# Attention with two passes: the maxima of later queries in the steps of the exponentials

## The chip, the cores and the metric

The kernel runs on one core of a Trainium2 chip. A core has a matrix engine (TensorE, PE in the profile), VectorE (DVE), ScalarE (ACT), GpSimd (POOL) and SyncE (SP, which only starts transfers here), each with its own stream of instructions; they work on an on-chip buffer, and TensorE writes to an accumulation memory of eight banks (PSUM) that VectorE and ScalarE read. The metric is the device time of one execution in microseconds (us), the median of some runs.

## The reference

Four layers, each a residual: group normalization of x, a mixing layer, and x plus its result. Only layer 0 is touched. x is (4, 96, 56, 56) in float32: four images of 96 channels and L = 3136 places.

```python
# layer 0, on tokens = normalized x as (4, 3136, 96); 3 heads of 16 dimensions
qkv = tokens @ w_qkv.T
q, k, v = ...                                    # (4, 3, 3136, 16) each
attn = softmax(einsum('bhnd,bhmd->bhnm', q, k) * 96 ** -0.5, axis=-1)
out = einsum('bhnm,bhmd->bhnd', attn, v)         # (4, 3, 3136, 16)
out = out.reshape(4, 3136, 48) @ w_proj.T + b_proj
```

Layers 1 and 3 are selective scans over image directions, layer 2 is an attention over windows. They are the larger part of the time, and their code is the same in both kernels.

## The kernel before, in words

`layer0` holds four images at once: image b lives on partitions 32b to 32b + 31 (`rows[b]`) of `qa` (queries) and `ka` (keys), as 16 dimensions and a row of ones in `ka`. Lines 136 to 153 load each image, normalize it (`group_norm`, lines 88 to 110) and compute the values of all heads into `va`, with ones beside them so that the sum of the weights comes out of the same product.

For each of the 3 heads there are then two stages, each with a PSUM pool of its own.

The stage of maxima (lines 160 to 196) first projects queries and keys in 7 chunks of 448 places (line 167). ScalarE takes the queries out of PSUM, VectorE the keys (171, 172), and POOL fills the row of ones (174). Then, for each of 25 tiles of 128 queries (the last has 64) and each of 7 chunks of 448 keys, four products (line 181, one per image) fill four banks, two to a tile `s`, and two reductions on VectorE (line 186) take the maximum over two banks each. Such a pair of a tile and a chunk is called a unit here: 175 per head. After seven units line 191 takes the maximum of the chunks into columns 0, 32, 64 and 96 of a cleared square (`mp`, cleared by POOL in line 190), a product with the identity (193) turns these columns into rows, and line 194 subtracts them from the query's row that meets the ones of the keys. From then on every score comes with its maximum taken away.

The stage of exponentials (lines 197 to 249) goes through 7 chunks of queries and 25 tiles of keys, 175 steps per head. A step has four score products (line 202, keys by queries, one bank per image, six banks in the pool), four exponentials on ScalarE (218) and four products with the values (223) that gather into one bank `acc`, image b on partitions `rows[b]`. After 25 steps lines 230 to 235 copy `acc`, spread the sums by a product with `perm`, take reciprocals and multiply. In the last head, lines 239 to 249 also apply the output projection for each image (three products, line 243), add bias and input, and store, both transfers on SP's queue.

All of this is written in program order. What runs beside what is decided by a scheduler that keeps the order of the program as priority, and by the buffers of the pools. `in_order` (line 54), which other layers use, chains the instructions of each engine in the order in which they are written.

Of the kernel before, what the change touches and what calls it, by code (L numbers as in the profile page):

```python
# [9 lines left out]
F32 = mybir.dt.float32  # L10
AF = mybir.ActivationFunctionType
ALU = mybir.AluOpType
AX = mybir.AxisListType
PSUM = bass.MemoryType.PSUM
# [3 lines left out]
L = H * W  # L18
# [13 lines left out]
def view(ap, offset, dims):  # L32

    return bass.AP(ap.tensor, ap.offset + offset, [ap.ap[0], *dims])
# [35 lines left out]
class Net:  # L70
# [41 lines left out]

    def layer0(self, xin, xout):

        nc, tc = self.nc, self.tc
        scale = C ** -0.5
        n128 = [(t * 128, min(128, L - t * 128)) for t in range((L + 127) // 128)]
        rows = [slice(32 * b, 32 * b + 32) for b in range(B)]
        with ExitStack() as cx:
            wp = cx.enter_context(tc.tile_pool(name="l0w", bufs=1))  # L120
            s1 = cx.enter_context(tc.tile_pool(name="l0b", bufs=1))
            ss = cx.enter_context(tc.tile_pool(name="l0s", bufs=2))
            psA = cx.enter_context(tc.tile_pool(name="l0pA", bufs=1, space=PSUM))
            psM = cx.enter_context(tc.tile_pool(name="l0pM", bufs=1, space=PSUM))
            wq, wk, wv, wo, bo, perm = (
                self.load(wp, n) for n in ("l0_wq", "l0_wk", "l0_wv", "l0_wo", "l0_bo", "k_perm")
            )

            def misc():
                return psM.tile([128, 512], F32, name="misc")  # L130

            xns = []

            va = s1.tile([128, len(n128), HEADS, B, 2 * HD], F32, name="va")
            nc.gpsimd.memset(va, 1.0)
            for b in range(B):
                x = s1.tile([C, L], F32, name="x")
                nc.sync.dma_start(x, xin[b])
                xn = s1.tile([C, L], F32, name=f"xn{b}")
                self.group_norm(x, xn, ss, psM, "misc")  # L140
                xns.append(xn)
                for t0 in range(0, len(n128), 8):
                    some = n128[t0 : t0 + 8]
                    n = some[0][1]
                    p = misc()
                    for i, (k0, nk) in enumerate(some):
                        nc.tensor.matmul(
                            p[:nk, i * 48 : (i + 1) * 48], xn[:, k0 : k0 + nk], wv, start=True, stop=True
                        )
                    nc.vector.tensor_copy(  # L150
                        va[:n, t0 : t0 + len(some), :, b, 0:HD],
                        p[:n, : 48 * len(some)].rearrange("p (t h d) -> p t h d", h=HEADS, d=HD),
                    )
            aos = []
            for h in range(HEADS):

                qa = s1.tile([128, L], F32, name="qa")
                ka = s1.tile([128, L], F32, name="ka")
                ao = s1.tile([128, L], F32, name=f"ao{h}")
                aos.append(ao)  # L160
                with tc.tile_pool(name="l0p1", bufs=3, space=PSUM) as ps:
                    for c in range(NCH):
                        cs = slice(c * CH, (c + 1) * CH)
                        p = ps.tile([128, 2, 512], F32, name="s")
                        for i, w in enumerate((wq, wk)):
                            for b in range(B):
                                nc.tensor.matmul(
                                    p[rows[b], i, :CH], w[:, 32 * h : 32 * h + 32], xns[b][:, cs],
                                    start=True, stop=True,
                                )  # L170
                        nc.scalar.copy(qa[:, cs], p[:, 0, :CH])
                        nc.vector.tensor_copy(ka[:, cs], p[:, 1, :CH])
                    for b in range(B):
                        nc.gpsimd.memset(ka[32 * b : 32 * b + 1, :], 1.0)  # L174

                    for q0, nq in n128:
                        pm = ss.tile([128, B, NCH], F32, name="pm")
                        for kc in range(NCH):
                            two = [ps.tile([128, 2, 512], F32, name="s") for _ in range(2)]
                            for b in range(B):  # L180
                                nc.tensor.matmul(  # L181
                                    two[b // 2][:nq, b % 2, :CH], qa[rows[b], q0 : q0 + nq],
                                    ka[rows[b], kc * CH : (kc + 1) * CH], start=True, stop=True,
                                )
                            for i in range(2):
                                nc.vector.tensor_reduce(  # L186
                                    pm[:nq, 2 * i : 2 * i + 2, kc], two[i][:nq, :, :CH], AX.X, ALU.max
                                )
                        mp = ss.tile([128, 128], F32, name="mp")
                        nc.gpsimd.memset(mp, 0.0)  # L190
                        nc.vector.tensor_reduce(view(mp[:nq], 0, [[32, B]]), pm[:nq], AX.X, ALU.max)
                        p = misc()
                        nc.tensor.matmul(p[:, :nq], mp[:nq, :], self.ident[:nq, :nq], start=True, stop=True)
                        nc.vector.tensor_tensor(
                            qa[:, q0 : q0 + nq], qa[:, q0 : q0 + nq], p[:, :nq], ALU.subtract
                        )
                with tc.tile_pool(name="l0p2", bufs=6, space=PSUM) as ps:

                    def scores(qc, k0, nk):
                        four = [ps.tile([128, 512], F32, name="s") for _ in range(B)]  # L200
                        for b in range(B):
                            nc.tensor.matmul(  # L202
                                four[b][:nk, :CH], ka[rows[b], k0 : k0 + nk],
                                qa[rows[b], qc * CH : (qc + 1) * CH], start=True, stop=True,
                            )
                        return four

                    todo = [(qc, t) for qc in range(NCH) for t in range(len(n128))]
                    s = scores(0, *n128[0])
                    for at, (qc, t) in enumerate(todo):  # L210
                        cs = slice(qc * CH, (qc + 1) * CH)
                        nk = n128[t][1]
                        if t == 0:
                            acc = psA.tile([128, 512], F32, name="acc")
                        es = []
                        for b in range(B):
                            e = ss.tile([128, CH], F32, name="e", bufs=8)
                            nc.scalar.activation(e[:nk], s[b][:nk, :CH], AF.Exp, scale=scale)  # L218
                            es.append(e)
                        if at + 1 < len(todo):  # L220
                            s = scores(todo[at + 1][0], *n128[todo[at + 1][1]])
                        for b in range(B):
                            nc.tensor.matmul(  # L223
                                acc[rows[b], :CH], va[:nk, t, h, b, :], es[b][:nk],
                                start=t == 0, stop=t == len(n128) - 1,
                            )
                        if t < len(n128) - 1:
                            continue
                        a = ss.tile([128, CH], F32, name="a")
                        nc.vector.tensor_copy(a, acc[:, :CH])  # L230
                        p = misc()
                        nc.tensor.matmul(p[:, :CH], perm, a, start=True, stop=True)
                        rc = ss.tile([128, CH], F32, name="rc")
                        nc.vector.reciprocal(rc, p[:, :CH])
                        nc.vector.tensor_tensor(ao[:, cs], a, rc, ALU.mult)
                        if h < HEADS - 1:
                            continue
                        for b in range(B):
                            x = ss.tile([C, CH], F32, name="xc")
                            nc.sync.dma_start(x, xin[b][:, cs])  # L240
                            p = misc()
                            for i in range(HEADS):
                                nc.tensor.matmul(
                                    p[:C, :CH], wo[rows[b], i, :], aos[i][rows[b], cs],
                                    start=i == 0, stop=i == HEADS - 1,
                                )
                            xo = ss.tile([C, CH], F32, name="xo")
                            nc.vector.scalar_tensor_tensor(xo, p[:C, :CH], bo, x, ALU.add, ALU.add)
                            nc.sync.dma_start(xout[b][:, cs], xo)


    def into_scan(self, xin, dram, orders):
# [1272 lines left out]
```

## Time and profile before

| what | value |
|---|---|
| median of 3 runs | 17090.54 us (17080.33 to 17101.61) |
| profiled execution | 17096.45 us |
| its span | 17094.7 us |
| granted TensorE clock, mean over the span | 0.877 of full speed |
| busy: PE, DVE, ACT, POOL | 78%, 82%, 72%, 45% of the span |
| line 186 (DVE), 1050 reductions | 1075.1 us, 1084 ns each |
| line 218 (ACT), 2100 exponentials | 975.8 us, 549 ns in the mean |
| line 181 (PE), 4200 rows | 1087.5 us, 922 ns each |

The span is the time from the first to the last instruction of one profiled execution. In the rows of a profile a float32 product appears as two matmul instructions, so the 4200 rows of line 181 are 2100 products. The matmuls' ends are modelled, and they overlap: the time between the starts of two groups says more about TensorE's pace than the length of a row. A row names output and inputs (`s<-ka,qa`), their shapes and the number of instructions merged into it. The granted clock is the share of its full clock that TensorE was given.

### The profile page before, as it was taken

The numbers are of one execution on the slowest core, as the hardware profiler recorded it, in microseconds if no ns is written. First come the engines' busy times: TensorE is split into PE (matmuls) and PEld (weight loads), VectorE is DVE, ScalarE is ACT, GpSimd is POOL, SyncE is SP. The second block draws the span as 40 slices with busy tenths as digits, with TensorE's granted clock in tenths as the row PEclk, the third lists the DMA queues.
The fourth block names the chain that finished last, engine by engine and source line by source line (L and its number), as shares of the span: only waits on it lengthen the run. The fifth ranks groups of instructions, "written<-read, shape, count | busy, mean of one in ns | idle before, by whom it ended". The sixth has DMA issues, their size and how long they took to land.

```text
span 17094.7 us, 498049 instructions
## 1 busy us (share of the span) xinstructions
PE 13251.9 (78%) x220632; PEld 8905.3 (52%) x220632; DVE 13981.4 (82%) x13756; ACT 12242.0 (72%) x16242; POOL 7703.0 (45%) x4069
## 2 busy tenths in 40 slices
PE   8999992777777777777777667838888888888844
PEld 4333430666666666666666444516666656666622
DVE  7271806999999999999999677768888888888887
ACT  0607063999999999999999234438888888888822
POOL 0000002988888888888888000003333333333300
PEclk6969685999999999999999578959999999999966
DMA  0000003343444444334444830032222212212122
GB/s 13 1 1 1 1 20 133 93 96 89 96 103 105 107 97 94 91 91 102 101 107 101 196 79 12 10 82 50 50 50 52 50 49 51 49 49 50 45 64 65
DMA packets 823179, 1152.29 MB, mean 67 GB/s; under 512 B 309360, under 2 KB 731408, under 8 KB 809248
## 3 DMA queue, kind: packets, MB, share of 16 engines
q1 hardware_dynamic: 763680, 1067.42, 25.7%
q10 hardware_dynamic: 53312, 38.55, 1.0%
q8 instruction: 1734, 28.41, 0.7%
q0 software_dynamic: 4032, 14.46, 0.3%
q14 instruction: 421, 3.45, 0.1%
HBM read 842.93 MB, written 277.18 MB: 66 GB/s over the span
## 4 chain that ended last, share of the span: by engine, by line
DVE 35%; PE 25%; ACT 17%; issue 15%; DMA 4%; POOL 2%; SPq 0%; DVEq 0%; ACTq 0%; POOLq 0%
DVE q L463 17%; PE q L1156 6%; DVE pm L186 6%; ACT ht L488 5%; PE s L202 4%; DVE cv L333 3%; ACT e L451 3%; PE acc L223 3%; ACT phi L1104 2%; PE z L1096 2%; DVE w L1144 2%; ACT w L1112 2%; PE t L386 2%; PE y L500 2%; PE t L479 1%
## 5 line engine op out<-in xcount | busy, mean ns | idle before, releaser
L443 POOL TENSOR_TENSOR q<-du,bm 128x1792 f32<-128x1792 f32 x1344 | 5348.8, 4026 | 2.9 <-DMA bm<-bc 2.9
L463 DVE TENSOR_TENSOR_SCAN q<-e,state,q 128x448 f32<-128x448 f32 x4608 | 4873.9, 1121 | 143.7 <-ACT e L451 142.0
L451 ACT ACTIVATE e<-dl,na 128x448 f32<-128x448 f32 x5376 | 3355.4, 640 | 177.2 <-DVE q L463 120.9
L500 PE MATMUL y<-ht,cd 128*32 128x64 f32 x75264 | 1837.2, 225 | 1479.4 <-ACT ht L488 1478.6
L479 PE MATMUL t<-ident,q 128*128 128x128 f32 x18816 | 2610.7, 292 | 93.8 <-issue 77.7
L1156 PE MATMUL q<-w,m 32*32 32x192 f32 x52224 | 2582.7, 348 | 116.3 <-DVE phi L1165 67.8
L479 PEld LDWEIGHTS t<-ident,q 128*128 128x128 f32 x18816 | 2377.1, 203 | 324.9 <-issue 202.1
L488 ACT COPY ht<-t 128x896 f32<-128x896 f32 x2688 | 2428.3, 903 | 88.9 <-PE t L479 59.5
L500 PEld LDWEIGHTS y<-ht,cd 128*32 128x32 f32 x75264 | 1399.8, 110 | 1956.2 <-ACT ht L488 1942.2
L1156 PEld LDWEIGHTS q<-w,m 32*32 32x32 f32 x52224 | 1876.4, 113 | 733.9 <-issue 163.3
L1165 DVE TENSOR_TENSOR phi<-q,phi 128x768 f32<-128x768 f32 x1632 | 1512.4, 951 | 549.7 <-PE q L1156 535.4
L1177 POOL TENSOR_TENSOR t<-t 128x384 f32<-128x384 f32 x408 | 407.2, 998 | 3002.5 <-DVE t L1176 2996.4
L218 ACT ACTIVATE e<-s 128x448 f32<-128x448 f32 (+1 forms) x2100 | 975.8, 549 | 1055.3 <-PE s L202 1025.2
L1096 PE MATMUL z<-ad,sm 32*32 32x256 f32 x39168 | 1278.5, 391 | 396.9 <-ACT phi L1104 382.7
L1104 ACT COPY phi<-z 128x1536 f32<-128x1536 f32 x816 | 1164.5, 1427 | 538.9 <-PE z L1096 538.9
L1144 DVE TENSOR_TENSOR w<-w,misc 128x3072 f32<-128x3072 f32 x408 | 1364.8, 3345 | 83.6 <-PE misc L1128 46.3
L1112 ACT ACTIVATE w<-phi,lntiny,w_k_rmask 128x3072 f32<-128x3072 f32 x408 | 1203.1, 2949 | 2.6
L186 DVE TENSOR_REDUCE pm<-s 128x2 f32<-128x896 f32 (+1 forms) x1050 | 1075.1, 1084 | 117.2 <-PE s L181 117.2
L1120 ACT ACTIVATE phi<-phi,w_k_nmask 128x3072 f32<-128x3072 f32 x408 | 1165.5, 2857 | 2.4
L181 PE MATMUL s<-ka,qa 32*128 32x448 f32 (+1 forms) x4200 | 1087.5, 922 | 22.2 <-POOL ka L174 17.6
L1096 PEld LDWEIGHTS z<-ad,sm 32*32 32x32 f32 x39168 | 709.0, 105 | 659.8 <-ACT phi L1104 466.6
L230 DVE COPY a<-acc 128x448 f32<-128x448 f32 x21 | 13.1, 624 | 997.5 <-PE acc L223 997.5
(250 smaller groups left out, 17464.3 us busy)
## 6 DMA issues: line engine op xcount, KB each, us to landing
bm<-bc SPq DMA_DIRECT2D x896, 448.0 KB
cm<-cd SPq DMA_DIRECT2D x544, 186.0 KB
l1y<-out SPq DMA_DIRECT2D x672, 96.0 KB
l1y<-out SPq DMA_DIRECT2D x672, 72.0 KB
y<-l1y ACTq DMA_DIRECT2D x224, 168.0 KB
l3y<-y SPq DMA_DIRECT2D x1616, 23.2 KB
w<-l3cr SPq DMA_DIRECT2D x408, 48.0 KB
l3cr<-phi SPq DMA_DIRECT2D x408, 48.0 KB
```

What stands on the lines that cost most here:

```text
L186: nc.vector.tensor_reduce(pm[:nq, 2 * i : 2 * i + 2, kc], two[i][:nq, :, :CH], AX.X, ALU.max)
L443: nc.gpsimd.tensor_tensor(q, spread(s["du"][:, j, :], ng), s["bm"][g], ALU.mult)
L451: nc.scalar.activation(e[:, :CH], s["dl"][:, j, :], AF.Exp, scale=na[:, s["k"], j, n : n + 1])
L463: nc.vector.tensor_tensor_scan(a, e, a, first, ALU.mult, ALU.add)
L479: nc.tensor.transpose(flat(t)[:, 128 * c : 128 * c + 128], view(q, h * NC2 + c, [[NC, 128]]), self.ident,)
L488: nc.scalar.copy(t, flat(s["t", j, g, h])[:, : NC2 * 128])
L500: nc.tensor.matmul(s["y", j][r : r + 32, c // 4, 64 * half : 64 * half + 64], s["cd"][:, half, g, c, :], s["t", j, g, h][:, 128 * i + 64 * ...
L1096: nc.tensor.matmul(z[32 * b : 32 * b + 32, p, dh].rearrange("p n d -> p (n d)"), s["s"][ps_, dh, b, lo : lo + 32], st["ad"][ps_, dh, 8 * h ...
L1112: nc.scalar.activation(w.rearrange("p a n d -> p (a n d)"), st["phi"].rearrange("p a b n d -> p (a b n d)"), AF.Sigmoid, bias=lntiny, scal ...
L1144: nc.vector.tensor_tensor(st["w"], st["w"], ut, ALU.mult)
L1156: nc.tensor.matmul(qp[bs, n, :DI], st["m"][bs, 4 * q + n, :], st["w"][bs, :, 4 * q + n, :], start=True, stop=True,)
L1165: nc.vector.tensor_tensor(ph, view(st[q], 0, [[256, 4], [32, 6], [1, 32]]), ph, ALU.mult)
```

## The change

Both stages of a head become one sequence of steps that runs through all heads. `units` lists the units (head, tile of queries, chunk of keys) and `steps` the steps (head, chunk of queries, tile of keys), 525 of each. The loop takes unit number i in the same turn as step number i - 32 (`LEAD`), so 32 turns have units alone, and the last 32 steps have no units. A turn has two halves. In the first, images 0 and 1 have the score products of the next step and images 2 and 3 those of the unit; then come two exponentials, two reductions and two gathering products for images 0 and 1. In the second half the images are exchanged.

The maxima are taken over single banks (four reductions of 448 elements in place of two of 896). PSUM is divided into four banks for exponentials (`psE`), three for everything else (`psM`) and one for `acc`. `qa` and `ka` have two buffers each, and the chunks of the next head's projection are spread over seven steps, four apart, towards the end of the head before. Both evacuations of a projection are on ScalarE; the row of ones comes in as a bias (`one`). The two squares `mp` are cleared once, by VectorE. The values are computed in the leading turns and copied by ScalarE. The end of a chunk (`finish`) is spread over later steps: sums to ScalarE's copy `tot`, the reciprocal in four pieces, one per step. The output goes out on POOL's queue; images 1 and 3 are loaded on ScalarE's queue. The whole sequence after the normalizations is under `in_order`.

```diff
...
+        LEAD = 32
...
+            psE = cx.enter_context(tc.tile_pool(name="l0pE", bufs=4, space=PSUM))
+            psM = cx.enter_context(tc.tile_pool(name="l0pM", bufs=3, space=PSUM))
...
+            one = wp.tile([128, 1], F32, name="one")
+            nc.vector.memset(one, 0.0)
             for b in range(B):
...
+                nc.vector.memset(one[32 * b : 32 * b + 1], 1.0)
+            mps = [wp.tile([128, 128], F32, name=f"mp{i}") for i in range(2)]
+            for mp in mps:
+                nc.vector.memset(mp, 0.0)
+            for b in range(B):
+                x = s1.tile([128, L], F32, name="x", tag="qa", bufs=2)
+                (nc.sync if b % 2 == 0 else nc.scalar).dma_start(x[:C], xin[b])
...
+            def values(b, t0):
...
+                p = psE.tile([128, 512], F32, name="s")
...
+            def project(h, c):
...
+                p = bank(), bank()
+                for i, w in enumerate((wq, wk)):
+                    for b in range(B):
                         nc.tensor.matmul(
...
+                            p[i][rows[b], :CH], w[:, 32 * h : 32 * h + 32], xns[b][:, cs],
+                            start=True, stop=True,
+                        )
+                nc.scalar.copy(qas[h][:, cs], p[0][:, :CH])
+                nc.scalar.activation(kas[h][:, cs], p[1][:, :CH], AF.Identity, bias=one)
...
+            def scores(u, bs):
...
+                for b in bs:
+                    p = bank()
+                    nc.tensor.matmul(
+                        p[:nq, :CH], qas[h][rows[b], q0 : q0 + nq],
+                        kas[h][rows[b], kc * CH : (kc + 1) * CH], start=True, stop=True,
+                    )
...
+            def largest(u, bs, ps):
...
+                for b, p in zip(bs, ps):
+                    nc.vector.tensor_reduce(
+                        pms[h, t][:nq, b : b + 1, kc], p[:nq, :CH], AX.X, ALU.max
+                    )
...
+            def into_row(u):
...
+                p = bank()
+                nc.tensor.matmul(p[:, :nq], mps[t % 2][:nq, :], self.ident[:nq, :nq], start=True, stop=True)
+                q = qas[h][:, q0 : q0 + nq]
+                nc.vector.tensor_tensor(q, q, p[:, :nq], ALU.subtract)
...
+            def weigh(s, bs):
...
+                for b in bs:
+                    p = sc[s, b] = psE.tile([128, 512], F32, name="s")
+                    nc.tensor.matmul(
+                        p[:nk, :CH], kas[h][rows[b], k0 : k0 + nk],
+                        qas[h][rows[b], qc * CH : (qc + 1) * CH], start=True, stop=True,
+                    )
...
+            def gathered(s, bs):
...
+                for b in bs:
+                    nc.tensor.matmul(
+                        sc["acc"][rows[b], :CH], va[:nk, t, h, b, :], sc[s, b][:nk],
+                        start=t == 0, stop=t == NT - 1,
+                    )
...
+            def finish(h, qc):
...
+                nc.vector.tensor_copy(a, sc["acc"][:, :CH])
+                yield
+                p = bank()
+                nc.tensor.matmul(p[:, :CH], perm, a, start=True, stop=True)
+                tot = ss.tile([128, CH], F32, name="tot")
+                nc.scalar.copy(tot, p[:, :CH])
+                yield
+                for i in range(4):
+                    r = tot[:, 112 * i : 112 * i + 112]
+                    nc.vector.reciprocal(r, r)
+                    yield
+                nc.vector.tensor_tensor(aos[h][:, cs], a, tot, ALU.mult)
+                yield
...
+                    nc.vector.scalar_tensor_tensor(xs[b], p[:C, :CH], bo, xs[b], ALU.add, ALU.add)
+                    nc.gpsimd.dma_start(xout[b][:, cs], xs[b])
+                    yield
+
+            with in_order(tc):
+                for c in range(NCH):
+                    project(0, c)
...
+                for at in range(-LEAD, len(steps)):
+                    u = units[at_u] if at_u < len(units) else None
+                    at_u += 1
+                    s = steps[at] if at >= 0 else None
+                    new = steps[at + 1] if -1 <= at < len(steps) - 1 else None
+                    if s is None and parts:
+                        values(*parts.pop(0))
+                    for two, first in (((0, 1), True), ((2, 3), False)):
+                        other = (2, 3) if first else (0, 1)
+                        if new is not None:
+                            weigh(new, two)
+                        if u is not None:
+                            ps = scores(u, other)
+                        if new is not None:
+                            exps(new, two)
+                        if u is not None:
+                            largest(u, other, ps)
+                        if s is not None:
+                            gathered(s, two)
+                    if ended is not None:
+                        into_row(ended)
+                        ended = None
+                    if u is not None and u[2] == NCH - 1:
+                        of_tile(u)
+                        ended = u
+                    next(done, None)
...
+                    if t == NT - 1:
+                        done = finish(h, qc)
+                        next(done)
+                    r = at % (NCH * NT) - (NCH * NT - LEAD - 5 * NCH)
+                    if h < HEADS - 1 and r >= 0 and r % 4 == 0 and r < 4 * NCH:
+                        project(h + 1, r // 4)
...
```

## Prediction, before the result was known

> **What bounds the kernel now.** The change touches the attention layer alone, so I first cut its stretch out of the page. The rows of tile `s` put it between 0 and about 2619 us: in each of three heads a stage of maxima (lines 176 to 196), then a stage of exponentials (197 to 249). The chain of waits asked for 0 to 2700 us says who sets its end:
>
> ```profile
> by line: DVE pm L186 35.6%; PE s L202 22.8%; PE acc L223 17.8%; PE s L181 6.0%; PE misc L243 3.7%; PE s L167 2.0%; PE misc L193 1.9%; PE misc L147 1.6%; DVE cv L333 1.0%; POOL ka L174 0.9%; issue 0.9%; DVE gn_st L93 0.8%; DVE rc L234 0.8%;
> ```
>
> In the maxima VectorE is the chain (line 186), in the exponentials TensorE (lines 202 and 223). Busy time by stretch, with the granted clock as the second last but one figure, shows the same:
>
> ```profile
> core 0: us, PE busy (x) PEld busy (x) DVE busy (x) ACT busy (x) POOL busy (x), PEclk, DMA share, GB/s
> ...
> 280.00:420.00 140.00, 130.84 (x513) 58.00 (x509) 130.66 (x143) 0.00 (x0) 1.63 (x8) 0.61 0.00 1
> ...
> 600.00:700.00 100.00, 100.00 (x784) 30.01 (x782) 8.41 (x6) 90.25 (x196) 0.00 (x0) 1.00 0.00 1
> ```
>
> ScalarE does nothing in the maxima, VectorE next to nothing in the exponentials: work to be put side by side. But TensorE is busy in both. The timeline gives the pace of each (start, length, engine, work):
>
> ```profile
> 399.12 3.17 PE L181 MATMUL s<-ka,qa 32*128 32x448 f32 x14
> 399.13 4.08 DVE L186 TENSOR_REDUCE pm<-s 128x2 f32<-128x896 f32 x4
> ...
> 602.85 3.71 ACT L218 ACTIVATE e<-s 128x448 f32<-128x448 f32 x8 [0.27 <-PE s L202]
> ...
> 700.53 1.03 PE L202 MATMUL s<-qa,ka 32*128 32x448 f32 x8
> 701.49 0.96 PE L223 MATMUL acc<-e,va 128*32 128x448 f32 x8
> 702.38 1.30 PE L202 MATMUL s<-qa,ka 32*128 32x448 f32 x8
> ```
>
> A reduction of two banks takes 4.08/4 = 1.02 us, so a unit of maxima (a tile of queries against one chunk of keys, four images) takes 2.04 us. Eight exponentials in 3.71 + 0.27 us make 1.99 us per step of four. On TensorE four score products take 701.49 - 700.53 = 0.96 us and four gathering products 702.38 - 701.49 = 0.89 us, so 1.85 us of each step. (Every product is two instructions in these rows, hence x8.) First to last row, the three stages of maxima last 402, 406 and 405 us, those of exponentials 367, 368 and 515 us (the last with the output projection, line 243); with 128 us ahead and two projections of 14 us they make 128 + 1213 + 1250 + 28 = 2619 us.
>
> **The steps merged.** Each of 525 steps now holds four exponentials, four gatherings and the scores and four single-bank reductions of one unit. What each engine needs:
> - ScalarE: 4 x 0.464 (3.71/8) = 1.86 us.
> - VectorE: a single-bank reduction is not in the trace. Bounded below by half of 1.02, so 0.51, above by the copy of the same tile out of PSUM (line 230, 0.62 each); seven statistics over 448 elements run in 3.77, 0.54 each. I take 0.55: 2.2 us. The row work (0.18 + 0.28 every seventh step) and the endings (0.62 + 2.96 + 0.62 in every 25) add 0.24: 2.5 us.
> - TensorE decides. The order of the code is, twice per step: two scores of the next step (images 0, 1), two of the unit (images 2, 3), two gatherings. The four scores still lie in four row strips and can run at once: 0.96 us. The gatherings go in twos.
>
> Does a pair take half of four? The timeline has one product alone and four together, both at half clock:
>
> ```profile
> 24.00 1.70 PE L167 MATMUL s<-xn,w_l_wq 96*32 96x448 f32 x2
> ...
> 103.36 1.73 PE L167 MATMUL s<-xn,w_l_wk 96*32 96x448 f32 x8
> ```
>
> One takes as long as four. So a pair of gatherings is 0.89 us, not 0.45, and the step is 2 x (0.96 + 0.89) = **3.70 us**, TensorE bound. Were pairs worth half, it would be 2.82. The merging thus saves not min(2.04, 1.99) but, of the 4.03 us that a unit and a step cost now, 0.33 us; the larger part of the gain is in what stands around.
>
> A rule that speaks against the change is in the Trainium skill, TensorEngine Tiling (Array Packing), Key Properties: a change of tiling mode drains TensorE. Scores (32 rows by 128 columns) and gatherings (128 by 32) are different modes, and the changes per step go from two to four. The row has the drain in it: two streams of a product are 2 x 0.37 us (half of the 0.747 us between starts of line 243 at half clock), 1.49 us for scores and gatherings, against 1.85 measured: 0.36 us per pair of changes. Without it the step would be 2.98 us and 378 us more would be won; I use the row.
>
> **The sum for the layer.**
> - Start. Normalizations of four images: the first input lands at 12 us; VectorE needs 3.78 + 0.34 + 0.15 + 0.15 + 0.21 + 0.16 + 1.91 = 6.7 us each, 27 us in all; images 2 and 3 wait for a buffer and 8 us of transfer (the first took 4.0 to 12.0). Estimate 50 us.
> - First projections: 112 instructions; 70 took 10.07 us before: 16 us. ScalarE's two evacuations (2 x 0.53 per chunk) hide behind them. ACT's row of ones by bias replaces POOL's 2.7 us fills.
> - 32 leading units with the values between: at least 32 x 2.2 = 70 us for VectorE; twelve groups of values at 2.0 (full clock) or 3.65 us (half) add 24 to 44 where they stand ahead of scores. With three banks, a bank's turn at half clock (1.75 + 0.62 + 0.11) gives 3.3 us a unit, 106 + 44 = 150. Between 94 and 150 I take 110. Steps begin at 176 us; the maxima began at 128.
> - 525 x 3.70 = 1943 us.
> - Rows of maxima: 70 x 0.42 = 29. Sums: 20 x 0.9 (a 448-column product) = 18. Output projections: 24 x 6 x 0.4 = 58 (they serve one row strip each, nothing overlaps); before, each took 5.6 us and waited for its VectorE step, 28 of them being most of the 150 us by which the third stage is longer. Projections for heads 1 and 2: 14 x 1.6 = 22; before 28 bare. Together 127 us.
> - Tail: copy 0.6, sum 0.9, ScalarE 0.5, reciprocals 3.0, product 0.6, four projections 9.6, last addition 0.7, output 2: 18 us.
>
> End: 176 + 1943 + 127 + 18 = 2264 us against 2619: **355 us less**. The profiled execution took 17096 us, 6 over the median of 17090.5; from the median that is 17,090.5 - 355 = 16,735 us, taken as **16,740**. The later layers I leave as they are.
>
> **Waits added.** Three banks serve four reductions per step. The second score of each half waits for the first reduction of the half before, and behind it on TensorE stand the gatherings. Counted from the start of gatherings: scores complete at +0.06, VectorE starts at +0.12 (0.055 us lie between end and start in the maxima), ends at +0.74, TensorE sees it at +0.80; it wants the bank at +0.89. So nothing is lost, with 0.09 us to spare. POOL and SP carry only transfers here: 28 outputs move from SP's queue to POOL's, whose fills are gone; the input loads stay on SP, four buffers ahead. Both are covered by 4 us per image; uncovered, only the last costs, some 2 us.
>
> **Rivals.**
> 1. *The bank wait decides* (17%). If the reduction comes 0.1 to 0.5 us late at each half-step, 1050 halves give back 105 to 525 us. For it: the margin of 0.09 and reciprocals (0.74 each) in front of reductions. Against: these stand in one step of five. Mean case 0.2 us, 210 us back: 16,945.
> 2. *TensorE is not granted its clock* (11%), slower. In the maxima it got 0.61 although busy 131 of 140 us. At that clock a step is 3.70/0.61 = 6.1 us, 1240 us more, 17,975. The change loses from 355/525 = 0.68 us per step on, a clock of 0.85. The Trainium skill, TensorE: Matmul & The Clock Gate (What's actually happening) has full clock after some 3.4 us of sustained activity and half after an idle window; by it alone an always busy TensorE has 1.0, whereas the maxima's row shows that busy records don't suffice: there products waited for VectorE at every pair. The exponentials' row, the same mix of products without gaps, shows 1.00; half-empty gatherings are the doubt. Against that, the last layer's small products (32*32, lines 1156 and 1096) keep 0.9.
> 3. *TensorE does better* (9%): pairs overlap across the mode changes, step near 3.2: 16,475.
> 4. *Nothing gained* (3%): steps near 4.3, within 0.2% (34 us, about what a measurement can tell).
>
> **How the numbers follow.** My case has 60%: steps of 3.55 to 3.85 (79 us either way) and a start of 94 to 150 us: its own range 16,640 to 16,840. The range of 8 in 10 adds most of rival 1: 16,640 to 16,980. Faster: 60 + 16 + 9 = 85%; same 4%; slower 11%.
>
> **What would show it.** Right: layer ending near 2264 us; gatherings x4 of about 0.9 us; step of 3.7; clock 0.95 or more from 200 us on; VectorE near 65% and ScalarE near 50% there. Wrong: scores waiting for VectorE in every half (rival 1), clock under 0.85 (2), gathering pairs of 0.5 us (3), or later layers that don't simply move up.

## The result and the profile after

The changed kernel takes **16,856.7 us** (median of four, 16,845.9 to 16,926.4) against 17,094.6 us of the kernel before, measured beside it: a ratio of 0.987, 95% interval 0.9843 to 0.9898. It is faster by 238 us; 355 were forecast. (Measured twice more, it was faster by 193 and 204 us.) The profiled execution took 16,926.4 us, the longest of the four, 170 us less than the profiled one before. The twelve executions of these three measurements fall into two groups: five at 16,846 to 16,866 us and seven at 16,902 to 16,930. All three traces are of the second group, so the sums below are made against those. What probably makes the two groups comes out below.

The chain of waits of the changed kernel from 0 to 2500 us:

```profile
by line: PE s L237 39.8%; PE acc L255 37.9%; PE m L197 9.2%; PE m L287 2.7%; PE s L160 1.6%; PE m L179 1.4%; PE m L227 1.3%; DMA x<-in_x 0.8%; PE m L267 0.8%; issue 0.8%; DVE gn_st L93 0.5%; DVE pm L210 0.5%; DMA x<-x 0.5%; DVE cv L425 0.4%
```

VectorE's maxima were 35.6% of the chain and are 0.5% now: TensorE sets the pace from end to end, by the scores (237 for the exponentials, 197 for the maxima) and the gatherings (255). One half-step on the timeline, weight loads left out:

```profile
699.39 0.65 PE L237 MATMUL s<-qa,ka 32*128 32x448 f32 x2
699.40 0.64 PE L197 MATMUL m<-ka,qa 32*128 32x448 f32 x2
699.87 0.54 PE L237 MATMUL s<-qa,ka 32*128 32x448 f32 x2
699.88 0.54 PE L197 MATMUL m<-ka,qa 32*128 32x448 f32 x2
700.35 0.95 PE L255 MATMUL acc<-e,va 128*32 128x448 f32 x4
700.44 0.98 ACT L246 ACTIVATE e<-s 128x448 f32<-128x448 f32 x2 [0.86 <-PE m L197]
700.52 1.16 DVE L210 TENSOR_REDUCE pm<-m 128x1 f32<-128x448 f32 x2 [0.68 <-PE m L197]
701.23 0.65 PE L237 MATMUL s<-qa,ka 32*128 32x448 f32 x2
701.24 0.64 PE L197 MATMUL m<-ka,qa 32*128 32x448 f32 x2
```

Two scores of a step and two of a unit start within 0.02 us of each other: they run at once. (At 699.87 us the second instruction of each float32 product follows.) From scores to gatherings it is 0.96 us, from gatherings to scores 0.88 us, a half-step of 1.84 us. A pair of gatherings costs what four cost before. Two reductions take 1.16 us and end 0.45 us after TensorE has gone on. The stretches, again with the granted clock second last but one:

```profile
core 0: us, PE busy (x) PEld busy (x) DVE busy (x) ACT busy (x) POOL busy (x), PEclk, DMA share, GB/s
66.00:229.00 163.00, 152.50 (x447) 86.74 (x449) 71.62 (x130) 7.80 (x17) 0.00 (x0) 0.51 0.00 0
...
700.00:1000.00 300.00, 299.77 (x1846) 76.69 (x1842) 184.71 (x330) 148.99 (x303) 0.00 (x0) 1.00 0.00 1
2240.00:2296.00 56.00, 56.00 (x242) 14.15 (x238) 6.13 (x11) 27.89 (x57) 0.00 (x0) 1.00 0.00 1
2296.00:2422.00 126.00, 126.00 (x295) 27.14 (x294) 2.27 (x4) 33.34 (x68) 2.05 (x4) 0.50 0.04 11
```

In the middle, VectorE is busy 62% and ScalarE 50% of the time and the clock is full. But the leading turns (66 to 229 us) and most of the end (from 2296 us on) run at half clock, with TensorE busy 94% and 100% of the time. A leading turn with values in it looks like this, from one group of scores to the next:

```profile
79.27 1.87 PE L197 MATMUL m<-ka,qa 32*128 32x448 f32 x6
81.84 1.86 PE L197 MATMUL m<-ka,qa 32*128 32x448 f32 x2 [0.70 <-DVE pm L210]
83.63 3.65 PE L160 MATMUL s<-w_l_wv,xn 96*128 96x48 f32 x16
87.21 1.87 PE L197 MATMUL m<-ka,qa 32*128 32x448 f32 x6
```

Three scores (x6) fill the three banks. The fourth waits for VectorE and costs nearly as much as the three, and then come the values: 7.94 us in all. The two stretches at half clock are where most of the missing gain went, together with a third thing that a stretch of 300 us does not show: from gathering to gathering some steps of the middle take 4.56 us and some 5.45, not 3.68. Half-steps of 2.72 us, in place of 1.84, make them, one or two in a step. Here is one:

```profile
515.70 0.95 PE L255 MATMUL acc<-e,va 128*32 128x448 f32 x4
516.57 0.97 PE L237 MATMUL s<-qa,ka 32*64 32x448 f32 x4
517.47 1.02 PE L197 MATMUL m<-ka,qa 32*128 32x448 f32 x4
518.42 0.94 PE L255 MATMUL acc<-e,va 128*32 128x448 f32 x4
```

The last tile of keys has 64 places, so its scores have 64 columns (`32*64`). They do not run beside the unit's scores of 128 columns, though they use other row strips of the array: 0.90 us for the one pair, then 0.95 for the other, where 0.96 had been enough for both.

### The profile page after: what moved, and what is told of

Same layout as the page of the kernel before. It is cut to its first block, busy times and chain, and to the rows that moved or that the text cites. A ratio compares the mean times of both kernels' runs of the same rounds, so it can differ in the third digit from the quotient of the medians.

```text
span 16924.6 us, 498034 instructions
## 1 busy us (share of the span) xinstructions
PE 13192.5 (78%) x220632; PEld 8680.7 (51%) x220632; DVE 14110.1 (83%) x14839; ACT 12324.2 (73%) x16300; POOL 7670.4 (45%) x4010
## 4 chain that ended last, share of the span: by engine, by line
PE 31%; DVE 28%; ACT 18%; issue 17%; DMA 3%; POOL 2%; SPq 0%; DVEq 0%; ACTq 0%; POOLq 0%
DVE q L555 16%; PE q L1248 6%; PE s L237 6%; PE acc L255 6%; ACT ht L580 5%; ACT e L543 4%; DVE cv L425 3%; ACT phi L1196 2%; PE z L1188 2%; DVE w L1236 2%; PE y L592 2%; PE t L571 2%; PE t L478 2%; ACT w L1204 1%; PE m L197 1%
## 5 line engine op out<-in xcount | busy, mean ns | idle before, releaser
L1248 PE MATMUL q<-w,m 32*32 32x192 f32 x52224 | 2579.2, 348 | 115.6 <-DVE phi L1257 66.5
L210 DVE TENSOR_REDUCE pm<-m 128x1 f32<-128x448 f32 (+1 forms) x2100 | 1211.9, 619 | 807.1 <-PE m L197 800.2
L246 ACT ACTIVATE e<-s 128x448 f32<-128x448 f32 (+1 forms) x2100 | 1027.5, 540 | 1162.3 <-PE m L197 820.6
L197 PE MATMUL m<-ka,qa 32*128 32x448 f32 (+1 forms) x4200 | 1134.0, 612 | 10.5 <-DVE pm L210 10.5
L237 PE MATMUL s<-qa,ka 32*128 32x448 f32 (+1 forms) x4200 | 1111.5, 600 | 0.0
```

The source lines that it names most:

```text
L237: nc.tensor.matmul(p[:nk, :CH], kas[h][rows[b], k0 : k0 + nk], qas[h][rows[b], qc * CH : (qc + 1) * CH], start=True, stop=True,)
L1248: nc.tensor.matmul(qp[bs, n, :DI], st["m"][bs, 4 * q + n, :], st["w"][bs, :, 4 * q + n, :], start=True, stop=True,)
```

## The experiments

The theory from these rows: the regular step is as forecast, and three losses were counted too low or not foreseen: (a) the lead at half clock, (b) the end at half clock, (c) the narrow last tile. The rivals: that waits for banks or the endings of the chunks make these stretches long, or that the difference lies in later layers.

**The same kernel again**, twice, for the two groups of times.

> The changed kernel once more, for a second trace. Theory: the 525 steps keep 3.68 us wherever the clock is full, and what differs between executions is when TensorE loses and gets its clock: in the last 32 steps (score products and gatherings in pairs alone; 6.87 us per step at half clock in the first trace) and in the leading turns (66 to 229 us there, at half clock). Then an execution of about 16,850 us has full clock for longer in one of the two, some 70 us in all, and the rest of the layer agrees within 10 us. Rival: the difference lies in the later layers, and the layer ends near 2440 us in every trace.

> The changed kernel again, beside the next two on one chip. Both traces of it lost TensorE's clock in the end at about 2297 us and had it back in the steps at 235 to 241; 16,850 to 16,920 us, the layer ending near 2440 if the clock is lost in the end, near 2385 if not.

Medians 16,909.0 us (ratio to before 0.9888, 0.9873 to 0.9902) and 16,887.5 us (0.9882, 0.9861 to 0.9903); profiled executions 16,916.1 and 16,916.0 us. Both traces again lose the clock near the end, at 2299 us (2296 in the first trace), get it back from the lead at 234 us (241), and end the layer at 2430 us (2439). The middle of the steps (25 to 450) takes 1712.6 us in each of the three traces, within 0.1 us. What the faster group looks like was therefore not seen directly.

**Filling the end.** The 32 last steps, which have no unit, compute two scores of an old unit in each half, which nobody reads:

```diff
                         if u is not None:
                             ps = scores(u, other)
+                        elif new is not None:
+                            scores(units[-8], other)
```

> In the last 32 steps, which have no unit, the two score products of a unit are issued all the same into the three banks, and nobody reads them: useless work on the two row strips that stand empty. Theory (the clock falls because half of the array stands empty): the clock stays at 1.0 to the end, the last steps take 3.68 us instead of 6.87, the layer ends near 2365 us instead of 2440, and the time is 16,800 to 16,850 with a small spread. Rival (clock has nothing to do with it, the steps are slow from the waits of the endings and output projections): no gain, or a loss of up to 10 us.

16,856.6 us (0.9857, 0.9842 to 0.9872), 7 us above the range given, four times within 16,852.5 to 16,864.7: 52 us less than the unfilled kernel measured beside it, by doing more work. Its stretches at the end:

```profile
2240.00:2290.00 50.00, 50.00 (x312) 12.68 (x312) 5.47 (x10) 24.97 (x51) 0.00 (x0) 1.00 0.00 1
2290.00:2340.00 50.00, 50.00 (x298) 14.76 (x292) 2.72 (x4) 21.73 (x45) 2.05 (x4) 1.00 0.10 28
```

The clock stays at 1.00 where it fell to 0.50 before; the last 32 steps take 127 us instead of 174 to 180. TensorE's records have no gap in either kernel, so it is not idle time that loses the clock here; what the edit adds is work on the half of the array that stood empty. The times are those of the faster group of the unfilled kernel. That this group is the executions that keep the clock in the end is the likely reading; no trace of one was had.

**Joining the end.** The last steps take their four scores, four exponentials and four gatherings at once, as the kernel before did:

```diff
...
-                    p = sc[s, b] = psE.tile([128, 512], F32, name="s")
+                    p = sc[s, b] = bank() if len(bs) == B and b > 1 else psE.tile([128, 512], F32, name="s")
...
-                    for two, first in (((0, 1), True), ((2, 3), False)):
-                        other = (2, 3) if first else (0, 1)
+                    halves = ((0, 1), (2, 3)) if u is not None else ((2, 3, 0, 1),)
+                    for two in halves:
+                        other = tuple(b for b in range(B) if b not in two)
...
```

> In the last 32 steps the halves are joined: four scores (two in banks of each pool), four exponentials, four gatherings. Theory (a pair on TensorE costs as much as four, so that the last steps cost 3.68 us at full and 6.87 at half clock for nothing): about 2.0 us per step as in the exponentials before the change, 64 us in place of the 183 us of the first trace, so 16,740 to 16,790 us. If pairs cost half of four, nothing is to be won but the clock: 16,800 to 16,850.

16,796.9 us (0.9821, 0.9806 to 0.9836), 112 us less than the changed kernel measured beside it. The 32 steps take 69 us, against 174 and against the 127 of the filled end. The time is 7 us above the range given. Four gatherings in these steps:

```profile
2250.02 0.54 PE L237 MATMUL s<-qa,ka 32*128 32x448 f32 x2
2250.49 0.99 PE L255 MATMUL acc<-e,va 64*32 64x448 f32 x8
2251.41 0.64 PE L237 MATMUL m<-qa,ka 32*128 32x448 f32 x2
```

0.92 us for four (x8), 0.88 for two (x4) above: the price of a pair, in one kernel and the other.

**The wide lead.** The leading turns issue four scores of a unit at once, two in each pool's banks, and the values after them:

```diff
...
-                    if s is None and parts:
-                        values(*parts.pop(0))
+                    if s is None and new is None:
+                        ps = scores(u, (2, 3))
+                        ps += scores(u, (0, 1), lambda: psE.tile([128, 512], F32, name="s"))
+                        if parts:
+                            values(*parts.pop(0))
+                        largest(u, (2, 3, 0, 1), ps)
...
```

> In the leading turns the four scores of a unit go out together, two in banks of each pool, and the values after them, so that VectorE's reductions run beside the values. The rest is unchanged. Theory (the lead is long because scores in pairs wait for three banks and TensorE runs at half clock, 2.57 us of waiting and work per three reductions): lead near 32 x 2.4 us and less cold, 80 to 110 us in place of 163, so 55 to 80 us less than the changed kernel: 16,780 to 16,800. Rival (the values on TensorE at half clock set the length, 12 x 3.65 us plus scores 1.8 per unit): 110 to 120 us of lead, 40 to 50 us less.

16,763.2 us (0.9802, 0.9786 to 0.9819). From the first unit to the first gathering it is 82 us instead of 169. The stretches of its lead:

```profile
64.00:100.00 36.00, 36.00 (x299) 26.62 (x298) 27.07 (x50) 6.47 (x14) 0.00 (x0) 1.00 0.00 1
100.00:146.00 46.00, 41.99 (x185) 20.80 (x182) 43.92 (x86) 4.37 (x10) 0.00 (x0) 0.74 0.00 1
```

While the values are computed the clock is full, and afterwards VectorE is busy 43.92 of 46 us: now it is its reductions that set the lead, as they should. The gain, 146 us below the changed kernel measured beside it, is larger than expected because in this trace the end keeps its clock too (its last 32 steps take 121 us), untouched by the edit. So losing the clock in the end is not certain, only frequent.

**Both together**, the edits of the last two experiments in one kernel.

> Both remedies together: units four at a time in the leading turns, and joined halves in the last 32 steps. Theory (two separate losses): the gains add up where the clock does not give one of them for nothing. Lead 82 us as in the run with the wide lead, end 69 us as in the run with joined halves (there 121 us at full clock in the wide lead's trace), so about 50 us less than the wide lead alone: 16,700 to 16,725 us. If the losses were one, 16,750 to 16,765.

16,718.2 us (0.9779, 0.9763 to 0.9795): in the range for separate losses. Lead 82 us, end 69 us.

**What pairs of gatherings cost in the middle.** All four gatherings once per step, with 3 banks for exponentials and 4 for the rest:

```diff
                         if new is not None:
-                            weigh(new, two)
+                            weigh(new, two[:1])
                         if u is not None:
                             ps = scores(u, other)
+                        if new is not None:
+                            weigh(new, two[1:])
...
-                        if s is not None:
-                            gathered(s, two)
+                        if s is not None and first:
+                            gathered(s, tuple(range(B)))
```

> All four gatherings once per step, between the halves; the pools have 3 banks for exponentials and 4 for the rest, and of each half's two scores for the exponentials one goes last. The question is what the gatherings in pairs cost. By the prediction's rule a pair costs 0.88 us like four, so TensorE's need falls from 3.68 to 0.95 + 0.95 + 0.89 = 2.8 us per step; but two groups of scores then stand back to back and want eight banks where there are seven, so the last score of one group in two waits for an exponential (0.08 + 0.54 us after the scores' end), which gives 2.8 + 0.65 = 3.45 us, 115 us less over 525 steps: about 16,750 to 16,800. If a pair cost half of four, the step would not fall below 3.68. If the banks were no matter: 2.8 us, VectorE (2.5) near its limit, 460 us less: 16,450.

16,807.2 us (0.9833, 0.9816 to 0.9851), 7 us above the range given, with four executions between 16,780 and 16,839. The regular step is 3.54 us: 0.14 better, where the count gave 0.23, and far from 2.8. So the gathering in one piece wins little: as the count says, seven banks are not enough for two groups of scores back to back, and a gathering spread over both halves fills time that would be lost anyhow. And part of the gain is lost again through the clock, here in the middle of the layer:

```profile
300.00:700.00 400.00, 399.19 (x2655) 127.33 (x2647) 254.81 (x471) 214.10 (x435) 0.00 (x0) 0.98 0.00 1
700.00:1100.00 400.00, 399.07 (x2430) 126.14 (x2426) 243.10 (x449) 197.18 (x401) 0.00 (x0) 0.93 0.00 1
1100.00:1500.00 400.00, 399.38 (x2395) 121.34 (x2392) 231.16 (x426) 194.54 (x394) 0.00 (x0) 0.91 0.00 1
```

Steps 25 to 450 take 1689.8 us, only 23 less than the changed kernel's 1712.6, where 425 x 0.14 is 60. The clock is lost mostly in one place of each head, among the seven steps with the units of the 64-wide tile, from 687, 1383 and 2107 us on for 61 to 68 us: such a step takes 10.4 us here, against 5.45 in the changed kernel at full clock. A larger part of the gain in time comes from elsewhere: with the fourth bank for the units the lead is 110 us instead of 169.

**Two banks in place of three** for the units' scores and all else in that pool (`bufs=3` to `bufs=2`).

> Two banks instead of three for the units' scores (and everything else of that pool), nothing else. This measures how near the bank wait of the prediction's first rival is. By its count from the start of the gatherings, the first bank is free at +0.80 and the second at +1.33 us, and TensorE wants both at +0.89: the second score waits 0.45 us in each half with a unit, 986 x 0.45 = 440 us, and the lead grows by about 60: 17,350 to 17,450 us. If the wait is smaller than counted: below 17,200. If both banks come late: above 17,600.

17,164.6 us (1.0041, 1.0026 to 1.0056): slower than the kernel before, but less than counted. The step is 4.17 us, so a half waits 0.24 us in the mean and not 0.45. The gatherings of three halves in a row show that this is two different waits:

```profile
699.64 0.95 PE L255 MATMUL acc<-e,va 128*32 128x448 f32 x4
...
701.90 0.94 PE L255 MATMUL acc<-e,va 64*32 64x448 f32 x4
...
703.81 0.94 PE L255 MATMUL acc<-e,va 64*32 64x448 f32 x4
```

One half takes 2.26 us, 0.42 more than 1.84 and nearly what was counted; the next takes 1.91. The late score delays the gatherings too, so the reductions of the next half start ahead of its gatherings and are done in time for all but 0.08 us. The lead is 205 us, 36 more than with three banks, where 60 were counted. The mechanism of the first rival is there, and one bank less would have turned the change into a loss; with three it does not act. In the changed kernel's own list of waits from 0 to 2500 us (waiter, what it waited for, us in total, times, longest) the units' scores stand with

```profile
PEld m L197 <- DVE pm L210: 98.0, 105, 2.1
```

105 waits over 1050 halves of units, 37 of them in the lead. All are waits of weight loads (PEld), which overlap products; from 240 us on no score product itself waited for a reduction, and no such wait stands in the regular step shown above.

**One width.** Queries and keys stand in 3200 columns, the last 64 of them zeros, and both score products always load 128 columns; the extra results are not read:

```diff
...
-                    qas.append(s1.tile([128, L], F32, name="qa", bufs=2))
-                    kas.append(s1.tile([128, L], F32, name="ka", bufs=2))
+                    qas.append(s1.tile([128, NT * 128], F32, name="qa", bufs=2))
+                    kas.append(s1.tile([128, NT * 128], F32, name="ka", bufs=2))
+                    nc.gpsimd.memset(qas[h][:, L:], 0.0)
+                    nc.gpsimd.memset(kas[h][:, L:], 0.0)
...
-                        p[:nq, :CH], qas[h][rows[b], q0 : q0 + nq],
+                        p[:, :CH], qas[h][rows[b], q0 : q0 + 128],
...
-                        p[:nk, :CH], kas[h][rows[b], k0 : k0 + nk],
+                        p[:, :CH], kas[h][rows[b], k0 : k0 + 128],
...
```

> The changed kernel with the last tile of 64 places computed at the width of the others: queries and keys stand in 3200 columns, 64 of them zeros that POOL sets, and both score products load 128 columns always; the results of the extra columns are not read. Theory (in the traces a 64-wide group of scores runs after the 128-wide one of its half instead of beside it, 1.85 us in place of 0.95, in some 40 of 493 steps with units: 21 with a unit of the last tile, 19 or 20 with the last keys): 40 x 1.78 = 71 us less than the changed kernel in the same call. Rival (the longer steps come from the endings that stand in the same steps): within 10 us.

16,817.6 us (0.9838, 0.9817 to 0.986), 70 us less than the changed kernel measured beside it. Both have executions of two groups; group by group they are 74 and 75 us apart. In the traces of the two the last unit comes at 2168.0 us and not at 2236.6, although the steps start 1.6 us later: 70 us, where 71 were expected. The end, still in pairs, loses the clock here too. Around the same place as above, with the last keys:

```profile
515.95 0.64 PE L239 MATMUL s<-qa,ka 32*128 32x448 f32 x2
515.97 0.71 PE L199 MATMUL m<-ka,qa 32*128 32x448 f32 x2
...
516.99 0.94 PE L257 MATMUL acc<-e,va 64*32 64x448 f32 x4
```

The two pairs start together again. Loading twice the columns, half of them zeros, is the cheaper way.

**All three remedies**, the edits of one width, wide lead and joined end in one kernel.

> One width, wide lead and joined end together. If the three losses are separate: the 16,718 us of the two remedies less about 70: 16,640 to 16,660 us, the layer's end near 2180 us.

**16,645.3 us** (0.9739, 0.9723 to 0.9755), four executions within 16,642.8 to 16,648.0; the layer ends at 2165 us. The losses were separate, and this version beats both kernels: 2.6% below before, twice the gain of the change as it was made. Two groups of times are not seen here, nor with the end filled or joined alone, while the one-width kernel, whose end stays in pairs, has them. This speaks for the end in pairs as their cause; with four executions of each kernel it is not shown.

## Why the prediction was right, and where its size was off

Direction and range held, and so did the mechanism of the regular step: TensorE is the bound, at 3.68 us per step against 3.70 forecast; a pair of gatherings costs 0.88 us like four; the bank is in time with three buffers; the clock is full in the middle. That the range held was in part luck. The case with this mechanism alone was given 16,640 to 16,840 us, and 16,857 lies above it, as do 16,909 and 16,888 of the repeats; the wider range reached them because it made room for the bank wait, which did not come. What came instead are the three losses. The change saves in the profiled execution 2619 - 2439 = 180 us in the layer, not 355. By the steps of the sum, forecast against the profiled execution:

| step of the prediction | forecast | measured | what the runs show |
|---|---|---|---|
| start and first projections | 66 | 66 | the units begin at 66.5 us |
| 32 leading turns | 110 | 163 | half clock; 77 when the scores go out in fours |
| 525 steps and what stands among them | 2070 | 2194 | see below |
| tail | 18 | 16 | 2423 to 2439 us |
| end of the layer | 2264 | 2439 | |

- **The term of 110 us for the lead** was mis-sized by 53. Its two ends were 94 and 150, and the value taken lay near the warm one, while the cold one was right; even that was short by 13. At half clock 3.3 us were counted for a unit and 3.65 for values, 6.95 in all, and such a turn took 7.94: with values in between, the fourth score cannot share a round of banks with the next unit.
- **"525 x 3.70 = 1943 us" treated all steps alike.** Two kinds were not. Some 40 steps with a 64-wide product cost 1.78 us more each, 70 us in all (shown by the one-width run). I had written that a change of tiling mode drains TensorE and used its price between scores and gatherings, but overlooked that the last tile is a change of shape too, and one that stands in the middle of a half. In the kernel before all four scores of a unit or step had one width, so no trace of it showed the price.
- **The last 32 steps**, counted at 3.70 us, cost 180 us and not the 121 that they take at full clock in the wide lead's trace (127 in the filled end), because the clock falls: 59 us. As far as the runs show, rival 2 was right in its mechanism and wrong in its place: the doubt of "half-empty gatherings" holds where the scores stand in pairs too, that is in the lead and the end, and not in the middle (in the lead TensorE also stands still for 10 of 163 us). 70 + 59 are 129; with the regular steps at 3.68 (525 x 0.02 = 10 less) 119 of the 124 us are explained. What stands among the steps was sized well: in the one-width trace steps 25 to 450 take 1658 us, 94 more than 425 x 3.68, and the prediction's terms make 92 for this stretch (an estimate: 26 for rows of maxima, 15 for sums, 29 for output projections, 22 for projections).
- **Rival 1, the bank wait**, was counted at 0.45 us with two banks and measured 0.24 in the mean. With three nothing waits, but it is closer than forecast: VectorE starts 0.17 us after the gatherings (700.52 against 700.35) and not 0.12, which leaves some 0.04 of the 0.09 us.
- **The drain.** The prediction took 0.36 us for a pair of changes of mode. Not all of it stands at the changes: in the step shown above the second instructions of the scores start 0.48 us after the first, where a stream was counted at 0.37, and no mode changes between them. The sum used the row of the trace and is not affected; but by this row 2.98 us is too low for a step without changes of mode.
- **Rival 3** (overlap across mode changes) did not occur: 0.96 and 0.88 us, as before the change.
- The forecast from the median used the profile's difference; the medians differ by 238 us, the profiled executions by 170. With the end at full clock the layer would save 180 + 59 = 239. This agrees with the 238 if the faster group, where the median of the first measurement lies, is the one that keeps the clock.
- Later layers moved up unchanged: from the next layer's first normalization product to the end it is 14,462 us before and 14,474 after, and 14,451 to 14,476 in the other traces of this case.

The Trainium skill's rule for the clock (TensorE: Matmul & The Clock Gate, What's actually happening: full after a window of sustained activity, half after an idle one) was weighed with an "always busy TensorE", which by it alone keeps 1.0. The rows differ: from 2296 us on a TensorE without gaps had 0.50 for 126 us, and in the filled end, as free of gaps, it had 1.00. The measurement decides. These rows fit an activity that is counted by how much of the array is in use; that is inferred, and it cannot be the whole rule, as two traces kept the clock with the same pairs.

## What to carry to other kernels

Before merging two stages, count the matrix engine's groups, not the products: a group of two costs what a group of four costs, so splitting is free only where the time is needed for something else, here the turn of the banks. Treat the turns without a partner, at the start and at the end of a skewed loop, as stages of their own, with a form that fills the array; they took the larger part of the missing gain, 53 and 59 of 175 us. And give products that are to run at once one tile shape, by padding the last tile if need be. All of this was measured on this kernel alone.

## What was not expected of the hardware

- Score pairs of 64 and of 128 columns on different row strips run one after the other: 0.90 + 0.95 us instead of 0.96. One width saved 70 us.
- A TensorE without gaps was put to half clock where half of its array stood empty, in all three traces of the changed kernel and in that of one width, and was not where useless products filled it. The loss is not certain: at 2240 to 2296 us the same pairs ran at full clock, and the traces of the wide lead and of the two banks kept it to the end (121 us for the last 32 steps in both). Once lost, it did not come back while the pairs lasted (126 us). What decides in a given execution stays open; in the four traces it fell with output projections, which use a single row strip, among the steps, but the same projections stand in the two that kept it.
- Units ride free on TensorE: a step in pairs without a unit takes 3.65 us at full clock, with one 3.68.
